# Four graph layers on one core: results of L2 and L3 used one step later, with nine and ten row buffers

## The chip, the core and the metric

The kernel runs on one core of a Trainium2 chip. A core has five engines that each work through a list of instructions in order: TensorE (PE in the profile; its weight loads are a row of their own, PEld), VectorE (DVE), ScalarE (ACT), GpSimd (POOL) and SyncE (SP). They share SBUF, on-chip memory of 128 partitions, and PSUM, into which matmuls write. They wait for each other by semaphores, which the framework places from the tiles that an instruction reads and writes. The metric is the device time of one execution, in microseconds (us).

## The reference

Node features x (6250 x 256) pass through four layers, each with its residual: h = relu(layernorm(x)), x = x + layer(h). All four share a list of 100000 edges (src, dst), sorted by dst. Only the last two layers are touched, cut here to what matters:

```
# L2: attention with one head
h   = x @ Wn.T + bn ;  e = edge_attr @ We.T + be
a   = leaky_relu(sum((h[src] + e) * attn), 0.01)          # one logit per edge
w   = exp(a - max over the edges of the same dst)
out = relu( sum over edges of w * h[src] / sum of w )      # per dst

# L3: graph convolution, with self loops
norm = deg(src)**-0.5 * deg(dst)**-0.5
out  = relu( sum over edges of (x @ W)[src] * norm + b )   # per dst
```

L0 is attention with eight heads and a feed-forward part, L1 a filtered message sum.

## The kernel before

`fast()` is the path that runs; `slow()` is the other branch of an If, for edge lists with other spacing. Nodes are padded to 49 blocks of 128. Edges are padded to 98 groups of 1024, as 8 tiles of 128 edges (J = 8). Since edges are sorted by dst, the targets of group g lie in a window of 128 nodes that begins at 64 g - 32.

Each of the stages L0 to L3 loops over the groups. For a group, POOL issues 8 indirect DMAs (`gather`, L130): each fetches, for 128 edges, the row of the source node from a table in device memory (xt2 for L2, 258 columns; xt3 for L3, 256 columns). DVE makes 8 one-hot matrices that say which target each edge has: L1095 in L2, where each row is also scaled by the edge's weight, L1150 in L3. PE multiplies one-hots with rows and adds the 8 products up in PSUM (`sum_tiles`, L681): the window sum. ACT copies it to SBUF (L691 in L2, L1175 in L3). In `sum_block` (L699) PE adds the windows that touch a block of 128 nodes, up to four, with shifted identity matrices. `blocks_done(g)` says which blocks are complete with group g: one for each even g from 2 to 96 (block 47 for 96), and block 48 for g = 97.

In L2, the weight of an edge comes from three small DVE operations, L1088 to L1090 (`al`, which read a column of the gathered rows), and an exp on ACT (L1092). A finished block goes through `out2` (L1104 to L1110): divide by the sum of weights, relu on ACT, residual, layer norm with a square root on ACT (L126), all in turns between DVE and ACT. `turned2` transposes it on PE (L1116) with a relu on ACT (L1118). `table3_row` multiplies by W on PE (L1124), scales on ACT (L1125) and writes the block's rows to xt3 with a DMA from SP (L1126). The scaled rows of all blocks also stay in SBUF, as `rows3` in the buffer `big`. exp and sqrt are in different tables of ACT; a switch is an ACT_TABLE_LOAD instruction.

In L3, `end3` (L1156 to L1159) adds the block's own row from `rows3` (the self loop), scales, adds bias and residual, and SP writes the block to the output (L1161). Every gather of L3 may read any row of xt3, so the first has to wait until L2 has written all 49 blocks.

The order of work in both loops is written out by hand under `tc.manual_schedule()`: the order in the Python code is the order of each engine's list. Step g of L2 is: gathers of group g (the first four groups are issued ahead of the loop, and ahead of an If at L1078); block sums of the blocks that were complete with g - 1; `turned2` of those complete with g - 2; weights, exp and one-hot of g; `out2` of the block summed in this same step; window sum and copy of g; `table3_row`. L3 is the same with fewer parts, and the one-hot is made a step ahead. A tile pool hands out `bufs` buffers for a tag in turn, and a new user waits until all readers of the old content are done. Row buffers: 5 groups in L2, 6 in L3. One-hots: 2. PSUM: S (window sums) 2, T (block sums) 2, B (transposes) 2, C (rows of xt3) 1. L1 gathers into twelve slices of `big` and makes the gather wait for the window sum twelve groups back (`wait_for`, L1008).

## Time and profile before

| | |
|---|---|
| median of 6 runs | 4504.04 us (4502.95 to 4508.93) |
| the profiled execution, its own time | 4501.16 us |
| its span, first to last instruction | 4499.3 us |
| busy: PE, PEld, DVE, ACT, POOL | 68%, 53%, 47%, 14%, 68% of the span |
| L2's gathers | 2497.10 to 3482.96 us |
| L3's gathers | 3501.89 to 4484.81 us |
| mean granted clock of PE | 0.826 |

A group of instructions in the profile is written as: line, engine, operation, what it writes and reads, shape, count, then busy time in us, mean ns of one, idle time of the engine just before them, and what ended most of it. "issue" means that nothing the profile shows was waited for. In a timeline, each row is the start and the length in us, and the bracket is the idle time before it with its releaser. A tile's name stands without its buffer number. Rows that were merged carry the count (x8, x16); a matrix product of 32-bit numbers shows as two passes, so that a window sum of 8 products is 16 matmuls.

### The profile page before, as it was taken

The page shows a single profiled execution, that of the slowest core. Times are in us where ns is not written, and L with a number is a line of the kernel's source. Part 1 is how long each engine was busy: PE and PEld are TensorE (multiplying, and loading weights), DVE is VectorE, ACT ScalarE, POOL GpSimd, SP SyncE. Part 2 cuts the span into 40 slices and gives each one's busy share as a digit, 9 for nine tenths or more (in the row PEclk, how much of TensorE's full clock was granted, in tenths as well). Part 3 has the DMA queues.
Part 4 walks back from the last instruction along what each step waited for, and adds up shares of the span by engine and source line. Part 5 has one row for each costly group of instructions (what it writes and reads, how often), then busy time and mean ns, then how long its engine had stood idle before and what let it go on. Part 6 is the DMA issues. An engine that isn't in the chain of part 4 may idle for free. (4 is left out here: it accounts for less than half of the span.)

```text
span 4499.3 us, 42030 instructions
## 1 busy us (share of the span) xinstructions
PE 3063.5 (68%) x12132; PEld 2375.8 (53%) x12133; DVE 2104.4 (47%) x6391; ACT 619.4 (14%) x1559; POOL 3057.5 (68%) x3215
## 2 busy tenths in 40 slices
PE   7688888888797565656566566656566555666556
PEld 4377777777645444544454345445455444444444
DVE  5476655665524566766766333333333222222222
ACT  3211010010124100000000122222222000000000
POOL 0377777777501677777777577777777677777776
PEclk9888888888898778787878688888888788788888
DMA  3365555555500344444444344444444333333333
GB/s 105 113 180 168 162 157 162 162 163 160 156 1 14 110 129 126 123 127 124 126 126 116 87 112 113 112 113 113 111 113 110 97 112 111 112 112 111 112 112 101
DMA packets 258740, 536.78 MB, mean 119 GB/s; under 512 B 65096, under 2 KB 144966, under 8 KB 258502
## 3 DMA queue, kind: packets, MB, share of 16 engines
q0 software_dynamic: 137984, 364.28, 29.8%
q1 hardware_dynamic: 107750, 156.85, 11.5%
q10 hardware_dynamic: 12768, 12.85, 0.9%
q8 instruction: 105, 1.72, 0.2%
q14 instruction: 133, 1.09, 0.1%
HBM read 504.57 MB, written 29.15 MB: 119 GB/s over the span
## 5 line engine op out<-in xcount | busy, mean ns | idle before, releaser
L130 POOL DMA_INDIRECT vg<-xt,src_i x1568 | 1489.0, 950 | 520.9 <-issue 488.3
L681 PE MATMUL ps_S<-vg,oh 128*128 128x258 f32 (+1 forms) x3136 | 988.3, 484 | 780.3 <-DMA vg<-xt,src_i 410.1
L681 PEld LDWEIGHTS ps_S<-vg,oh 128*128 128x128 f32 x3136 | 762.7, 249 | 997.8 <-issue 393.4
L130 POOL DMA_INDIRECT xbuf<-vt,src_i x784 | 782.8, 999 | 241.0 <-issue 210.4
L130 POOL DMA_INDIRECT big<-ht,src_i x784 | 742.7, 947 | 245.1 <-issue 200.0
L681 PE MATMUL ps_S<-oh,big 128*128 128x128 f32 x1568 | 308.4, 377 | 334.7 <-DVE big L1026 271.5
L1150 DVE TENSOR_SCALAR oh<-iota,rel 128x128 f32<-128x128 f32 x784 | 166.6, 301 | 740.9 <-PE ps_S L681 738.6
L681 PE MATMUL ps_S<-xbuf,oh 128*128 128x265 f32 x1568 | 486.5, 476 | 13.1 <-issue 12.1
L681 PEld LDWEIGHTS ps_S<-oh,big 128*128 128x128 f32 x1568 | 285.9, 282 | 365.3 <-DVE big L1026 236.1
L681 PEld LDWEIGHTS ps_S<-xbuf,oh 128*128 128x128 f32 x1568 | 367.6, 241 | 98.9 <-issue 16.8
L763 PE MATMUL ps_A<-scw,to 128*128 128x16 f32 x1568 | 222.5, 285 | 118.7 <-DVE to L748 118.6
L763 PEld LDWEIGHTS ps_A<-scw,to 128*128 128x128 f32 x1568 | 219.1, 222 | 137.2 <-issue 92.2
L1095 DVE TENSOR_SCALAR oh<-iota,rel,ex 128x128 f32<-128x128 f32 x784 | 215.5, 371 | 143.0 <-ACT ex L1092 143.0
L699 PE MATMUL ps_T<-ws,shifts 128*128 128x265 f32 (+2 forms) x1164 | 278.7, 382 | 0.0
L691 ACT ACTIVATE ws<-ps_S 128x265 f32<-128x265 f32 (+1 forms) x196 | 76.5, 390 | 1222.2 <-PE ps_S L681 1222.2
L699 PEld LDWEIGHTS ps_T<-ws,shifts 128*128 128x128 f32 x1164 | 220.8, 190 | 33.6
L1026 DVE TENSOR_TENSOR big<-big,ps_A 128x384 f32<-128x384 f32 (+1 forms) x294 | 132.3, 505 | 222.1 <-DMA big<-ht,src_i 220.7
L836 DVE TENSOR_TENSOR xbuf<-xbuf,ps_E 128x2048 f32<-128x2048 f32 x98 | 223.6, 2281 | 23.7 <-ACT ps_E L774 23.7
L980 PE MATMUL ps_A<-wr,rb 99*128 99x384 f32 (+1 forms) x588 | 215.3, 507 | 9.9 <-DMA rb<-in_rbf 9.9
L1088 DVE TENSOR_TENSOR al<-vg,te 128x8 f32<-128x8 f32 x98 | 16.4, 168 | 428.6 <-DMA vg<-xt,src_i 428.6
L988 DVE TENSOR_SCALAR oh<-iota,rel,cut 128x128 f32<-128x128 f32 x784 | 212.3, 362 | 0.0
L900 POOL TENSOR_TENSOR xbuf<-xbuf,bout 128x1024 f32<-128x1024 f32 (+1 forms) x13 | 29.0, 2231 | 256.1 <-ACT xn L898 249.3
(226 smaller groups left out, 3050.0 us busy)
## 6 DMA issues: line engine op xcount, KB each, us to landing
drow<-in_dst_row SPq DMA_DIRECT2D x98, 512.0 KB
ea<-in_edge_attr SPq DMA_DIRECT2D x98, 512.0 KB
vg<-xt,src_i POOLq DMA_INDIRECT x1568, 2.8
xbuf<-vt,src_i POOLq DMA_INDIRECT x784, 2.8
big<-ht,src_i POOLq DMA_INDIRECT x784, 2.6
rb<-in_rbf SPq DMA_DIRECT2D x196, 49.5 KB
vt<-row SPq DMA_DIRECT2D x49, 132.5 KB
xt<-row SPq DMA_DIRECT2D x49, 129.0 KB
```

The lines of the kernel that those rows point to most:

```text
L130: return nc.gpsimd.indirect_dma_start(out=rows, out_offset=None, in_=table, in_offset=bass.IndirectOffsetOnAxis(ap=idx[:, j:j + 1], axis=0))
L681: m = wait_for(nc.tensor.matmul(s, l, r, start=j == 0, stop=j == len(pairs) - 1), made)
L691: nc.scalar.activation(ws, s, AF.Copy)
L699: nc.tensor.matmul(t, shift_by(s), sums[g], start=i == 0, stop=i == len(parts) - 1)
L763: nc.tensor.matmul(dgs[g][:, j, :], tos[g][:, j * P:(j + 1) * P], scw[:, g // 2, g % 2, :], start=True, stop=True)
L836: made_g = nc.vector.tensor_tensor(vals, vals, ex[:, :, :, None].to_broadcast([P, J, H, HD]), OP.mult)
L900: nc.gpsimd.tensor_tensor(x[:, b0:b1, :], x[:, b0:b1, :], w1["bout"][:, None, :].to_broadcast([P, b1 - b0, D]), OP.add)
L980: filtered[g] = nc.tensor.matmul(t, rbs[g][0:33 * n, g % 2, q, :], wr3[0:33 * n, 0:n, :], start=True, stop=True)
L988: nc.vector.tensor_scalar(ohs[g][:, j, :], iota, rel[:, c], w1["cut"][:, c], OP.is_equal, OP.mult)
L1026: made_g = nc.vector.tensor_tensor(hg[:, js, :], hg[:, js, :], t, OP.mult)
L1095: made_g = nc.vector.tensor_scalar(oh[:, j, :], iota, rel[:, g * J + j:g * J + j + 1], ex[:, j:j + 1], OP.is_equal, OP.mult)
L1150: made_g = nc.vector.tensor_scalar(oh[:, j, :], iota, rel[:, g * J + j:g * J + j + 1], None, OP.is_equal)
```

## The change

In L2, a step now handles: gathers of g + 1; block sum of the blocks complete with g - 2; transposes (g - 4); product with W (g - 6); weights and one-hot of g + 1; `out2` (g - 3); window sum of g; copy of the window sum of g - 1; relu of the transposed block (g - 5); scaled row and its DMA (g - 7). In L3: gathers of g; load of the own rows of the blocks complete with g; block sum (g - 2); window sum of g; one-hot of g + 2; copy of the window sum of g - 1; `end3` (g - 3).

Rows are gathered into a list of views: three groups (L2) or four (L3) in a tile of their own, and six in `big`. A gather that reuses a view is given a wait for the last matmul of that view's window sum. `rows3` no longer exists: a block's scaled row is a tile of its own, and L3 loads the own rows back from xt3 with SP. One-hots get 4 buffers, copied window sums 8, `xn` 2. PSUM in L2: S 3, T 2, B 2, C 1, and tag A is gone, for which a branch that is not run here uses B; in L3: S 4, T 3, in a pool of its own.

The diff's core:

```diff
+        in_pool2, in_pool3, ahead = 3, 4, 4
+            room2 = ep.tile([P, in_pool2, J, TR], F32, name="vg", bufs=1)
+            views = [room2[:, i] for i in range(in_pool2)]
+            views += [big[:, i * J * TR:(i + 1) * J * TR].rearrange("p (j t) -> p j t", j=J) for i in (3, 4, 5, 0, 1, 2)]
             def rows2(g):
+                i = g % len(views)
+                vgs[g] = views[i]
+                gots[g] = [wait_for(gather(vgs[g][:, j, :], xt2, src_i[:, g * J:(g + 1) * J], j),
+                                    *([ends[g - len(views)]] if g >= len(views) else []))
+                           for j in range(J)]
...
+            def summed(g, n):
+                if g < G:
+                    wins[g] = ps("S", [P, n])
+                    oh, made_g = ohs.pop(g)
+                    ends[g] = sum_tiles(wins[g], [(oh[:, j, :], vgs[g][:, j, :]) for j in range(J)],
+                                        made_g, gots[g])
+            def taken(ep, g, n):
+                if 0 <= g < G:
+                    sums[g] = ep.tile([P, n], F32, name="ws", bufs=8)
+                    nc.scalar.activation(sums[g], wins.pop(g), AF.Copy)
...
+            def row3(b, t):
+                row = ep.tile([P, D], F32, name="row3", bufs=3)
+                nc.scalar.activation(row, t, AF.Copy, scale=dinv[:, b:b + 1])
+                nc.sync.dma_start(xt3[b * P:(b + 1) * P, :], row)
...
+                one_hot2(0)
+                for g in range(G + 7):
+                    if ahead <= g + 1 < G:
+                        rows2(g + 1)
+                    for b in blocks_done(g - 2):
+                        blocks[b] = sum_block(sums, b, TR)
+                    for b in blocks_done(g - 4):
+                        turns[b] = turned2(normed.pop(b))
+                    for b in blocks_done(g - 6):
+                        cs[b] = table3_row(b, hbs.pop(b))
+                    one_hot2(g + 1)
+                    for b in blocks_done(g - 3):
+                        normed[b] = out2(b, blocks.pop(b))
+                    summed(g, TR)
+                    taken(ep, g - 1, TR)
+                    for b in blocks_done(g - 5):
+                        hbs[b] = ep.tile([P, 2, P], F32, name="hb")
+                        nc.scalar.activation(hbs[b], turns.pop(b), AF.Relu)
+                    for b in blocks_done(g - 7):
+                        row3(b, cs.pop(b))
...
+            one_hot3(0)
+            one_hot3(1)
+            for g in range(G + 3):
+                rows3_(g)
+                for b in blocks_done(g):
+                    owns[b] = ep.tile([P, D], F32, name="own", bufs=3)
+                    nc.sync.dma_start(owns[b], xt3[b * P:(b + 1) * P, :])
+                for b in blocks_done(g - 2):
+                    blocks[b] = sum_block(sums, b, D)
+                summed(g, D)
+                one_hot3(g + 2)
+                taken(ep, g - 1, D)
+                for b in blocks_done(g - 3):
+                    end3(b, blocks.pop(b))
```

More of the change, by code (lines that the diff above doesn't have):

```diff
@@ L333, in make_windows @@
             nc.vector.tensor_reduce(lohi[:, i, :], dstf, AX.X, op)
-            t = ps("A", [P, P])
+            t = ps("B", [P, P])
             nc.tensor.transpose(t[:G, :], lohi[:, i, :], ident)
@@ L1058, in fast @@
             nc.vector.tensor_scalar(te, te, w1["ba"], None, OP.add)
-        ps = fctx.enter_context(Psum("ps2", S=2, A=1, T=2, B=2, C=1))
+        psc2 = fctx.enter_context(ExitStack())
+        ps = psc2.enter_context(Psum("ps2", S=3, T=2, B=2, C=1))
         w3 = weights(wp, "L3_gnn_W", D, D)
         brow = on_all(wp, "L3_gnn_b", D)
-        bufs2, ahead = 5, 4
+        in_pool2, in_pool3, ahead = 3, 4, 4
         with tc.tile_pool(name="e2", bufs=2) as ep:
-            vgs, gots, sums, normed = {}, {}, {}, {}
+            vgs, gots, ohs, wins, ends, sums, blocks, normed = {}, {}, {}, {}, {}, {}, {}, {}
+            room2 = ep.tile([P, in_pool2, J, TR], F32, name="vg", bufs=1)
+            views = [room2[:, i] for i in range(in_pool2)]
+            views += [big[:, i * J * TR:(i + 1) * J * TR].rearrange("p (j t) -> p j t", j=J) for i in (3, 4, 5, 0, 1, 2)]
             def rows2(g):
-                vgs[g] = ep.tile([P, J, TR], F32, name="vg", bufs=bufs2)
-                gots[g] = [gather(vgs[g][:, j, :], xt2, src_i[:, g * J:(g + 1) * J], j) for j in range(J)]
+                i = g % len(views)
[3 more added lines that the diff above has]
+                           for j in range(J)]
             with tc.manual_schedule():
@@ L1084, in one_hot2 @@
             def one_hot2(g):
+                if g >= G:
+                    return
                 gs = slice(g * J, (g + 1) * J)
@@ L1092, in one_hot2 @@
                 nc.scalar.activation(ex, al, AF.Exp)
-                oh = ep.tile([P, J, P], F32, name="oh")
+                oh = ep.tile([P, J, P], F32, name="oh", bufs=4)
                 for j in range(J):
@@ L1096, in one_hot2 @@
                                                      ex[:, j:j + 1], OP.is_equal, OP.mult)
-                return oh, made_g
+                ohs[g] = oh, made_g
+            def summed(g, n):
[8 more added lines that the diff above has]
+                    nc.scalar.activation(sums[g], wins.pop(g), AF.Copy)
             def out2(b, s):
@@ L1108, in out2 @@
                 norm_stats(b, b + 1)
-                xn = ep.tile([P, D], F32, name="xn", bufs=1)
+                xn = ep.tile([P, D], F32, name="xn", bufs=2)
                 nc.vector.tensor_scalar(xn, x[:, b, :], mv[:, b, 0:1], rstd[:, b, :], OP.subtract, OP.mult)
@@ L1116, in turned2 @@
                     nc.tensor.transpose(t[:, k, :], xn[:, k * P:(k + 1) * P], ident)
-                hb = ep.tile([P, 2, P], F32, name="hb")
-                nc.scalar.activation(hb, t, AF.Relu)
-                return hb
+                return t
             def table3_row(b, hb):
@@ L1124, in table3_row @@
                     nc.tensor.matmul(t, hb[:, k, :], w3[:, k, :], start=k == 0, stop=k == 1)
-                nc.scalar.activation(rows3[:, b, :], t, AF.Copy, scale=dinv[:, b:b + 1])
-                nc.sync.dma_start(xt3[b * P:(b + 1) * P, :], rows3[:, b, :])
-            with tc.manual_schedule():
-                for g in range(G + 2):
-                    if ahead <= g < G:
-                        rows2(g)
-                    summed = [(b, sum_block(sums, b, TR)) for b in blocks_done(g - 1)]
-                    turned = [(b, turned2(normed[b])) for b in blocks_done(g - 2)]
-                    if g < G:
-                        oh, made_g = one_hot2(g)
-                    for b, s in summed:
-                        normed[b] = out2(b, s)
-                    if g < G:
-                        sums[g], _ = sum_window(ep, oh, vgs[g], TR, made_g, gots[g])
-                    for b, hb in turned:
-                        table3_row(b, hb)
@@ L1144, in fast @@
-        with tc.tile_pool(name="e3", bufs=2) as ep, tc.manual_schedule():
-            sums = {}
+                return t
+            def row3(b, t):
+                row = ep.tile([P, D], F32, name="row3", bufs=3)
+                nc.scalar.activation(row, t, AF.Copy, scale=dinv[:, b:b + 1])
+                nc.sync.dma_start(xt3[b * P:(b + 1) * P, :], row)
+            turns, hbs, cs = {}, {}, {}
+            with tc.manual_schedule():
+                one_hot2(0)
[18 more added lines that the diff above has]
+                        row3(b, cs.pop(b))
@@ new lines, in fast @@
+        psc2.close()
+        ps = fctx.enter_context(Psum("ps3", S=4, T=3))
+        with tc.tile_pool(name="e3", bufs=2) as ep, tc.manual_schedule():
+            sums, blocks, ohs, wins, vgs, gots, ends, owns = {}, {}, {}, {}, {}, {}, {}, {}
+            room3 = ep.tile([P, in_pool3, J, D], F32, name="vg", bufs=1)
+            views = [room3[:, i] for i in range(in_pool3)]
+            views += [big[:, i * J * D:(i + 1) * J * D].rearrange("p (j t) -> p j t", j=J)
+                      for i in range(2 * NACC // (J * D))]
@@ L1147, in one_hot3 @@
             def one_hot3(g):
-                oh = ep.tile([P, J, P], F32, name="oh")
+                if g >= G:
+                    return
+                oh = ep.tile([P, J, P], F32, name="oh", bufs=4)
                 for j in range(J):
@@ L1151, in one_hot3, with rows3_ @@
                                                      OP.is_equal)
-                return oh, made_g
+                ohs[g] = oh, made_g
+            def rows3_(g):
+                if g < G:
+                    vgs[g] = views[g % len(views)]
+                    gots[g] = [wait_for(gather(vgs[g][:, j, :], xt3, src_i[:, g * J:(g + 1) * J], j),
+                                        *([ends[g - len(views)]] if g >= len(views) else []))
+                               for j in range(J)]
             def end3(b, s):
                 r0, r1 = b * P, min(N, (b + 1) * P)
-                nc.vector.tensor_tensor(s, s, rows3[:, b, :], OP.add)
+                nc.vector.tensor_tensor(s, s, owns[b], OP.add)
                 nc.vector.scalar_tensor_tensor(s, s, dinv[:, b:b + 1], brow, op0=OP.mult, op1=OP.add)
@@ L1161, in end3 @@
                     nc.sync.dma_start(out[r0:r1, :], y[0:r1 - r0, :])
-            oh, made_g = one_hot3(0)
-            for g in range(G + 1):
-                if g < G:
-                    vg = ep.tile([P, J, D], F32, name="vg", bufs=6)
-                    got = [gather(vg[:, j, :], xt3, src_i[:, g * J:(g + 1) * J], j) for j in range(J)]
-                summed = [(b, sum_block(sums, b, D)) for b in blocks_done(g - 1)]
-                if g < G:
-                    s = ps("S", [P, D])
-                    sum_tiles(s, [(oh[:, j, :], vg[:, j, :]) for j in range(J)], made_g, got)
-                    if g + 1 < G:
-                        oh, made_g = one_hot3(g + 1)
-                    sums[g] = ep.tile([P, D], F32, name="ws", bufs=6)
-                    nc.scalar.activation(sums[g], s, AF.Copy)
-                for b, s in summed:
-                    end3(b, s)
+            one_hot3(0)
[12 more added lines that the diff above has]
+                    end3(b, blocks.pop(b))
     def slow():
```

## The prediction

> **What bounds the kernel now.** I read the page's groups first, then busy time by stretch, the list of waits of POOL, and the timeline where stages meet. L2 runs from its first gather at 2497.10 to 3482.96 us, L3 from 3501.89 to the end. In the groups, POOL's row gathers are the costliest:

> ```profile
> L130 POOL DMA_INDIRECT vg<-xt,src_i x1568 | 1489.0, 950 | 520.9 <-issue 488.3
> ```

> A gather occupies POOL for 950 ns, and nearly all its idle time has "issue" as cause: no result was missing. Busy time by stretch (length, then PE, PEld, DVE, ACT, POOL with counts, clock, DMA), 300 us out of L1, L2 and L3:

> ```profile
> 1700.00:2000.00 300.00, 180.97 (x780) 141.77 (x780) 205.43 (x510) 18.77 (x75) 226.98 (x240) 0.80 0.47 126
> ...
> 2700.00:3000.00 300.00, 187.13 (x689) 149.65 (x689) 108.77 (x435) 77.03 (x150) 227.03 (x240) 0.84 0.42 113
> ...
> 3700.00:4000.00 300.00, 179.77 (x593) 141.59 (x593) 70.46 (x284) 11.17 (x30) 227.11 (x240) 0.81 0.39 111
> ```

> Each holds 240 gathers: 1.25 us apiece, 10 us a group, whatever the other engines do (PE 60 to 62% busy). POOL's list of waits has only three over 0.3 us in L2 and L3: 22.2 us ahead of L2's first gather, 18.9 ahead of L3's, and 3.1 behind the If at L1078, where POOL waits for its own 32 gathers. So inside the stages nothing is to be gained by using results later, and row buffers are not short. What can move the time is the stretch from the last landing of L2 to the first gather of L3, and that from the last landing of L3 to the end. Both are chains without a gather beside them. L2's end:

> ```profile
> 3475.31 0.17 DVE L1090 TENSOR_TENSOR al<-al,shift 128x8 f32<-128x8 f32 x1
> 3475.56 1.28 ACT L1092 ACT_TABLE_LOAD   x1 [1.41 <-DVE al L1090]
> 3476.85 0.21 ACT L1092 ACTIVATE ex<-al 128x8 f32<-128x8 f32 x1
> ...
> 3485.92 0.20 ACT L1092 ACTIVATE ex<-al 128x8 f32<-128x8 f32 x1
> ...
> 3486.15 2.14 DVE L1095 TENSOR_SCALAR oh<-iota,rel,ex 128x128 f32<-128x128 f32 x8 [0.61 <-ACT ex L1092]
> ...
> 3488.35 3.75 PE L681 MATMUL ps_S<-vg,oh 128*128 128x258 f32 x16 [1.10 <-DVE oh L1095]
> ...
> 3493.44 0.16 DVE L1104 TENSOR_SCALAR rd<-ps_T 128x1 f32<-128x1 f32 x1 [2.10 <-PE ps_T L699]
> ...
> 3498.76 0.47 ACT L1125 ACTIVATE big<-ps_C,dinv 128x256 f32<-128x256 f32 x1 [1.22 <-PE ps_C L1124]
> ...
> 3501.89 0.97 POOL L130 DMA_INDIRECT vg<-xt,src_i  x1 [18.93 <-DMA xt<-big]
> ```

> Group 96 pays 1.28 us for a table load between its logits and its exp; group 97 (from 3485.92) does not. After group 97's window sum comes block 48's chain, its row is written, and only then does POOL gather. L3's end, PE alone:

> ```profile
> 4466.67 3.69 PE L681 MATMUL ps_S<-vg,oh 128*128 128x256 f32 x16 [1.94 <-DMA vg<-xt,src_i]
> 4476.74 6.57 PE L681 MATMUL ps_S<-vg,oh 128*128 128x256 f32 x16 [6.38 <-DMA vg<-xt,src_i]
> 4483.15 1.89 PE L699 MATMUL ps_T<-ws,shifts 128*128 128x256 f32 x8
> 4486.94 3.69 PE L681 MATMUL ps_S<-vg,oh 128*128 128x256 f32 x16 [1.90 <-DMA vg<-xt,src_i]
> 4490.47 1.46 PE L699 MATMUL ps_T<-ws,shifts 128*128 128x256 f32 x6
> ```

> The same 16 matmuls take 3.69 us after 1.9 us of idle and 6.57 after 6.38. Other pairs of the stage: idle up to 2.35, 3.69; 4.55 to 4.75, 5.38 to 6.1; over 6.2, 5.2 to 6.7.

> **The change, part by part.** Sums are against the profiled execution (span 4499.3, its own time 4501.16), 2.9 us under the median of 4504.04; I add to the median.

> *Row buffers, 9 and 10, and the gather's wait for the window sum 9 or 10 groups back.* Behind a waiting gather stand all later ones on POOL's queue, and DVE's logits wait for them. But nine groups are 90 us, and a window sum is done within some 20 us of its landing: it lies some 70 us back. L1 (L1008) waits in this very form, and its 240 gathers take the same 300 us: 0.

> *Steps apart, inside a stage.* The same instructions, now a step later; POOL's 10 us a group covers them: 0. If that cover were gone, a group would cost its PE work, 187.13 / 30 = 6.2 us: still less than 10. Where a stall between PE, DVE and ACT goes, POOL is late next, as before.

> *Own rows read back in L3:* 49 more loads of 128 KB on SP, 6.3 MB beside the some 109 MB the stage moves (983 us at 111 GB/s). The last two are issued at steps 96 and 97, ahead of the last stores: 0. The row writes of L2 stay 49.

> *PSUM tags, bufs, one branch's tag in code that isn't run here:* 0, but for C, below.

> *L2's end.* Zero is the start of al(97), 3484.97. Before: one-hot made by 3.33, PE starts at 3.38, out2(48) starts at 8.47, its xn ends at 11.59, row(48) ends at 14.26, L3's gather at 16.92. After:
> 1. The out2 of a block now follows the one-hot of an even group. So the odd group's exp comes behind out2's square root and needs the table load; 97 is odd. By group 96's rows the one-hot is done 4.42 after its al, against 3.33: +1.0 at PE.
> 2. PE's queue: window sum 97 from 4.4 (16 passes at 0.216, 3.46), then block 47's sum, which used to be ahead of it (8 passes, 1.73): ready at 9.8. DVE is done with out2(46) at 7.4. out2(47) takes 3.12 (3493.44 to 3496.56 for block 48), to 12.9. Block 48's sum (behind turned2(46) and table3_row(45)) is ready at 12.4, so out2(48) starts at 12.9, not 8.47: +4.4, the 1.0 included.
> 3. C has one buffer. At step 103 table3_row(48) must wait for row3(47) of that same step. PE turns xn(48) first (done 16.5), then multiplies block 47 (1.0), ACT takes it (0.5), then block 48's product and row: done 19.6, 3.1 after the turn, against 2.2: +0.95.

> L2's end: **+5.4**. Bounds: +1.0, if only the table load is late; +6.9, if PE's window sum 97 falls into the slow clock (5.26 instead of 3.75).

> *L3's end.* Block sums move from odd steps to even ones. Window 97 thus has no block sum between it and window 96: PE idles some 6.3 us before it, and window 96 gets the warm 3.69 instead. Window 97 then takes 5.2 to 6.7, mean of such rows 5.9: +2.2 (1.5 to 3.0). Behind it PE runs block 47's sum (1.73) before block 48's, and DVE end3(47) before end3(48): block 48's y would end 1.9 later. L3's end: **+4.1**, between +1.9 (clock warm) and +4.9.

> [...]

> Sum: 5.4 + 4.1 = **+9.5, 4513.5 us** (0.21%).

> *Not shown:* gathers are 942 ns at the shortest and 950 on average; 8 x 1568 = 12.5 us is stretch, and the long ones I looked at lie beside DVE's one-hot TENSOR_SCALARs (1.02 at 4009.84 beside L1150 from 4008.96). Phases may shift it: from -12.5 to about as much more. The one-hots keep number and trigger (landing in L2, a window's end in L3), so I take 0, nearest to the row, and allow 4.

> **Rivals.**
> *Both ends mostly absorbed.* DVE and ACT catch up, the blocks' sums are ready earlier than my queue order says: 1.0 + 1.9 remain, 4507. For it: PE is idle a third of the time. Against: each engine works its list in order.
> *Not slower: the stretch goes.* Place: POOL's gathers in L2 and L3; price: all 12.5 of them; 9.5 - 12.5 = -3, 4501. It decides from 9.5 of the 12.5 on. For it: one-hots run further ahead. Against: their trigger stays tied to landings. With the lower bounds of both ends as well (2.9) it would be -9.6, 4494.
> *Gather waits aren't hidden.* A semaphore instruction on POOL's queue lasts 17 ns at the median; one for each of 1416 gathers (89 and 88 groups of 8) is +24, with the ends 4537.5. For it: each gather is handed one more wait. Against: L1's pitch of 1.25.

> **How the numbers follow.** About 0.2% (9 us) is what a measurement of this kernel can tell from no change. Forecast 0.70 (its middle lies at that bound: slower 0.41, same 0.29); absorbed 0.09 (same); stretch goes 0.08 (same 0.06, faster 0.02); waits 0.08 (slower); something not seen 0.05 (faster 0.04, slower 0.01). Faster 0.06, same 0.44, slower 0.50. Range: from absorbed less 2 of stretch, 4505, to both upper bounds (6.9 + 4.9 = 11.8) plus 4, 4520; the waits' case and most of what is unseen stay out.

> **What would show it.** Right: POOL's pitch 1.25 in both stages; a table load ahead of ex(97); idle before L3's first gather about 24.3 instead of 18.9; L3's last window over 5 us; from the last gather's start to the last y 13.6 instead of 9.5. Wrong: a pitch other than 1.25, new waits of POOL on ps_S, or ends as long as now.

## The result and the profile after

The changed kernel takes 4513.85 us (median of 18 runs, 4509.14 to 4518.51) against 4503.91 (38 runs, 4500.32 to 4509.44): +9.9 us, ratio 1.0022, 95% interval 1.0016 to 1.0028, which is +7.2 to +12.6 us. The profiled execution has a span of 4513.2 us (4499.3 before) and a mean granted clock of 0.817 (0.826 before).

First, busy time by stretch of the changed kernel, 300 us out of L2 and out of L3 (length, then PE, PEld, DVE, ACT, POOL with counts, clock, DMA):

```profile
2700.00:3000.00 300.00, 193.28 (x690) 152.36 (x690) 107.33 (x433) 72.13 (x149) 227.21 (x240) 0.82 0.42 112
3700.00:4000.00 300.00, 181.40 (x599) 143.02 (x598) 71.28 (x285) 11.49 (x30) 226.91 (x241) 0.81 0.41 118
```

The gathers come at the same pace as before, 240 and 241 in 300 us. So the stages are nearly where they were, and the two stretches without gathers must hold most of the difference. Here is L2's end in the timeline of the changed kernel, from the last rows of group 97 to L3's first gather (start and length in us, in brackets the idle time before it and its releaser):

```profile
3490.61 1.28 ACT L1103 ACT_TABLE_LOAD   x1 [4.67 <-DVE al L1101]
...
3492.15 2.14 DVE L1106 TENSOR_SCALAR oh<-iota,rel,ex 128x128 f32<-128x128 f32 x8 [1.61 <-ACT ex L1103]
...
3494.35 3.75 PE L681 MATMUL ps_S<-big,oh 128*128 128x258 f32 x16 [0.82 <-DVE oh L1106]
...
3497.94 1.90 PE L699 MATMUL ps_T<-ws,shifts 128*128 128x258 f32 x8
...
3499.88 0.16 DVE L1129 TENSOR_SCALAR rd<-ps_T 128x1 f32<-128x1 f32 x1 [2.53 <-PE ps_T L699]
...
3502.80 0.15 DVE L1129 TENSOR_SCALAR rd<-ps_T 128x1 f32<-128x1 f32 x1
...
3507.78 1.13 PE L1147 MATMUL ps_C<-l_gnn_w,hb 128*128 128x256 f32 x4 [0.56 <-ACT row L1152]
...
3509.00 0.47 ACT L1152 ACTIVATE row<-ps_C,dinv 128x256 f32<-128x256 f32 x1 [1.27 <-PE ps_C L1147]
...
3512.13 0.95 POOL L130 DMA_INDIRECT vg<-xt,src_i  x1 [24.63 <-DMA xt<-row]
```

Read it from top to bottom: a table load now stands ahead of group 97's exp; block 47's sum (3497.94) comes behind window 97, so both `out2` of blocks 47 and 48 follow one another (3499.88 and 3502.80); block 48's product waits until ACT has taken block 47's row (3507.78, "ACT row L1152"). POOL's idle time ahead of L3 is 24.63 us instead of 18.93. And L3's end, PE alone:

```profile
4487.10 5.38 PE L681 MATMUL ps_S<-big,oh 128*128 128x256 f32 x16 [2.95 <-DMA big<-xt,src_i]
4497.28 5.83 PE L681 MATMUL ps_S<-big,oh 128*128 128x256 f32 x16 [4.80 <-DMA big<-xt,src_i]
4502.95 3.19 PE L699 MATMUL ps_T<-ws,shifts 128*128 128x256 f32 x14
```

The last window takes 5.83 us instead of 3.69, and the sums of blocks 47 and 48 (8 and 6 matmuls) are one run of 14 behind it. The last gather and the last y, before:

```profile
4483.87 0.95 POOL L130 DMA_INDIRECT vg<-xt,src_i  x1 [0.30 <-issue]
...
4492.96 0.43 DVE L1159 SCALAR_TENSOR_TENSOR y<-ps_T,xbuf 128x256 f32<-128x256 f32 x1
```

and after:

```profile
4494.14 0.95 POOL L130 DMA_INDIRECT big<-xt,src_i  x1 [0.30 <-issue]
...
4507.20 0.42 DVE L1209 SCALAR_TENSOR_TENSOR y<-ps_T,xbuf 128x256 f32<-128x256 f32 x1
```

From the last gather's start to the end of the last y there are now 13.48 us, 9.52 before.

The pieces of the span, read from the traces of all the runs that follow (us; "L2" and "L3" from the first to the last gather's start, "end 2" from there to L3's first gather, "end 3" from L3's last gather's start to the end of the span, L1 for comparison, since nothing in it differs):

| kernel | L1 | L2 | end 2 | L3 | end 3 | median, ratio to before (interval) |
|---|---|---|---|---|---|---|
| before | 980.47 | 984.92 | 19.87 | 981.98 | 15.48 | 4503.91 |
| after | 981.07 | 987.16 | 25.57 | 982.01 | 19.08 | 4513.85, 1.0022 (1.0016 to 1.0028) |
| l3_only | 980.04 | 983.92 | 22.15 | 980.81 | 18.67 | 4503.25, 1.0003 (0.9994 to 1.0012) |
| few_rows | 979.48 | 985.19 | 25.69 | 981.20 | 18.51 | 4510.24, 1.0019 (1.0010 to 1.0028) |
| short_ends | 981.30 | 986.46 | 27.03 | 981.75 | 18.45 | 4508.49, 1.0017 (1.0008 to 1.0026) |
| split_before | 980.00 | 984.75 | 19.51 | 980.84 | 12.45 | 4496.18, 0.9990 (0.9981 to 0.9999) |
| l2_only | 980.82 | 985.56 | 27.06 | 983.51 | 15.55 | 4508.92, 1.0019 (1.0010 to 1.0028) |
| split_after | 982.06 | 990.09 | 25.97 | 984.64 | 13.90 | 4503.24, 1.0006 (0.9997 to 1.0016) |
| old_ends | 982.05 | 989.30 | 24.27 | 986.26 | 17.30 | 4508.53, 1.0015 (1.0006 to 1.0024) |
| split_old | 980.50 | 985.71 | 22.45 | 983.51 | 12.53 | 4503.25, 1.0007 (0.9998 to 1.0016) |

A row's pieces are of one execution, its median is of 11 or more; the profiled executions of split_after, old_ends and short_ends were the longest of their kernels (4519.11, 4519.99 and 4512.91 us), that of l3_only the shortest (4498.55). The kernel before ran beside each: 4501.74 us beside the first four experiments, 4501.25 beside the next four.

### The profile page after: what moved, and what is told of

It is laid out like the page before. It is cut to its first block, busy times and chain, and to the rows that moved or that the text cites. A ratio compares the mean times of both kernels' runs of the same rounds, so it can differ in the third digit from the quotient of the medians.

```text
span 4513.2 us, 42114 instructions
## 1 busy us (share of the span) xinstructions
PE 3091.6 (69%) x12132; PEld 2393.2 (53%) x12133; DVE 2103.1 (47%) x6391; ACT 606.1 (13%) x1557; POOL 3061.3 (68%) x3215
## 5 line engine op out<-in xcount | busy, mean ns | idle before, releaser
L130 POOL DMA_INDIRECT big<-xt,src_i x984 | 936.2, 951 | 302.5 <-issue 287.5
L130 POOL DMA_INDIRECT xbuf<-vt,src_i x784 | 783.8, 1000 | 241.1 <-issue 210.6
L130 POOL DMA_INDIRECT big<-ht,src_i x784 | 743.3, 948 | 246.3 <-issue 198.5
L681 PE MATMUL ps_S<-big,oh 128*128 128x258 f32 (+1 forms) x1968 | 579.3, 459 | 277.5 <-DMA big<-xt,src_i 226.0
L130 POOL DMA_INDIRECT vg<-xt,src_i x584 | 555.1, 950 | 222.2 <-issue 192.4
L681 PEld LDWEIGHTS ps_S<-big,oh 128*128 128x128 f32 x1968 | 458.5, 237 | 401.2 <-issue 214.4
L681 PE MATMUL ps_S<-oh,big 128*128 128x128 f32 x1568 | 309.4, 378 | 332.8 <-DVE big L1026 304.7
L699 PE MATMUL ps_T<-ws,shifts 128*128 128x265 f32 (+2 forms) x1164 | 314.8, 408 | 279.8 <-ACT ws L1122 279.8
L681 PE MATMUL ps_S<-vg,oh 128*128 128x256 f32 (+1 forms) x1168 | 354.1, 470 | 214.7 <-DMA vg<-xt,src_i 183.9
L681 PE MATMUL ps_S<-xbuf,oh 128*128 128x265 f32 x1568 | 486.6, 476 | 12.6 <-issue 12.0
L681 PEld LDWEIGHTS ps_S<-oh,big 128*128 128x128 f32 x1568 | 286.2, 282 | 363.3 <-DVE big L1026 230.2
L681 PEld LDWEIGHTS ps_S<-vg,oh 128*128 128x128 f32 x1168 | 278.9, 243 | 291.3 <-issue 177.2
L681 PEld LDWEIGHTS ps_S<-xbuf,oh 128*128 128x128 f32 x1568 | 367.9, 241 | 98.2 <-issue 15.8
L699 PEld LDWEIGHTS ps_T<-ws,shifts 128*128 128x128 f32 x1164 | 225.7, 199 | 330.3 <-ACT ws L1122 298.9
```

The lines of the kernel that those rows point to most:

```text
L130: return nc.gpsimd.indirect_dma_start(out=rows, out_offset=None, in_=table, in_offset=bass.IndirectOffsetOnAxis(ap=idx[:, j:j + 1], axis=0))
L681: m = wait_for(nc.tensor.matmul(s, l, r, start=j == 0, stop=j == len(pairs) - 1), made)
L699: nc.tensor.matmul(t, shift_by(s), sums[g], start=i == 0, stop=i == len(parts) - 1)
```

## The experiments

The theory: POOL's pace sets the stages, so the change can only move the two ends, and there it costs what each engine's list now has in another order. The rivals: the new distance or the buffers cost something inside the stages; or longer gathers (VectorE's work beside them) are the cause. "Cold" or "slow" below means that PE had half its clock for all or part of a row (granted clock 0.50 in the profile, 1.00 when warm). The diffs show an experiment's main lines against the changed kernel, that of split_before against the kernel before.

### l3_only: L2 as before, L3 as changed

```diff
+                nc.scalar.activation(rows3[:, b, :], t, AF.Copy, scale=dinv[:, b:b + 1])
...
-                one_hot2(0)
-                for g in range(G + 7):
...
+                for g in range(G + 2):
+                    if ahead <= g < G:
+                        rows2(g)
+                    summed = [(b, sum_block(sums, b, TR)) for b in blocks_done(g - 1)]
```

> L2 as before (five row tiles, PSUM as before, rows of L3's table kept in SBUF), L3 as in the changed kernel. My theory (the price lies only in the two stretches without gathers): the idle time ahead of L3's first gather goes back to about 18.9 us (24.6 in the changed kernel), the tail from L3's last gather to the last y stays near 13.5 us (9.5 before); time against the kernel before +4.0 us, ratio 1.0009 (1.0004 to 1.0014), 4508. Rival A (the step distance or the buffers cost something inside the stages): the whole +9.9 stays, or half of it by gathers and not by ends, and L3's pitch is not 1.254 us. Rival B (the stretch of L2's gathers beside VectorE's normalising made the difference): +2 or less is given back beyond the end's 5.7.

Measured: +1.5 us by the medians, ratio 1.0003 (0.9994 to 1.0012); the expected +4.0 lies in that interval, and so does nothing at all. The traces are sharper. L3's tail is 18.67, close to the changed kernel's 19.08; the idle time ahead of L3's first gather is 21.2 and not 18.9, though L2 is as before. PE's rows say why, here the last products of L2 and the last window of L3:

```profile
3491.85 2.08 PE L1126 MATMUL ps_C<-l_gnn_w,hb 128*128 128x256 f32 x4 [0.53 <-ACT hb L1120]
...
4481.21 5.38 PE L681 MATMUL ps_S<-big,oh 128*128 128x256 f32 x16 [4.88 <-DMA big<-xt,src_i]
```

The four products of block 48 took 2.08 us; in the kernel before 1.13 after the same idle time of 0.53, at a granted clock of 1.00. In the changed kernel's trace such four products, with no idle time ahead, take 1.91 us at a clock of 0.50 (2601.57) and 1.03 at 1.00 (3506.19). Window 96 in L2 took 6.44 instead of 5.26. That is 2.1 of the 2.3 us, by an estimate from these rows the clock's, in another execution of the same instructions. So an end can't be told from one execution more closely than by some 2 us. L3, the changed stage here, takes 980.81 us, so rival A is not met for L3; this run says nothing yet about L2's new form.

### few_rows: fewer row views

```diff
-            views += [big[:, i * J * TR:(i + 1) * J * TR].rearrange("p (j t) -> p j t", j=J) for i in (3, 4, 5, 0, 1, 2)]
+            views += [big[:, i * J * TR:(i + 1) * J * TR].rearrange("p (j t) -> p j t", j=J) for i in (3, 4)]
...
-                      for i in range(2 * NACC // (J * D))]
+                      for i in range(2)]
```

> The changed kernel with five row views in L2 and six in L3 instead of nine and ten, nothing else. My theory (row buffers are never waited for, POOL's pitch sets the stages): the same time as the changed kernel within 2 us, 4514, ratio to before 1.0022 (1.0015 to 1.0029), pitch 1.254 us, no wait of POOL on PE. Rival (the longer distance of the steps needs the buffers): in L2 a group's window is summed one step after its one-hot, so with five views POOL would wait on PE for up to one step of 10 us per group; already 0.1 us per group in both layers would be +20 us, 4534 or more.

Measured: 1.0019 (1.0010 to 1.0028), level with the changed kernel's 1.0022; stages 985.19 and 981.20 us, ends as in the changed kernel (25.69 and 18.51). Among POOL's waits are the one ahead of L3's first gather and those for the window sums, of which none is longer than the normal step between two gathers (in us: in total, times, longest):

```profile
POOL vg L130 <- DMA xt<-row: 24.7, 1, 24.7
...
POOL big L130 <- PE ps_S L681: 5.5, 18, 0.3
POOL vg L130 <- PE ps_S L681: 4.9, 16, 0.3
```

The nine and ten row buffers are worth nothing here, and five and six cost nothing. The rival's 0.1 us a group is excluded.

### short_ends: the last groups in another order

```diff
-                for g in range(G + 7):
+                for g in range(G - 2):
...
+                summed(G - 2, TR)
+                relu_b(h - 3)
+                row3(h - 4, cs.pop(h - 4))
...
+                one_hot2(G - 1)
+                row3(h - 2, cs.pop(h - 2))
+                normed[h - 1] = out2(h - 1, blocks.pop(h - 1))
```

(h is block 48; L3's last group is put in the order of the kernel before in the same way.)

> The changed kernel inside both layers (one step later everywhere, nine and ten views), but for the last two groups of L2 and the last group of L3 the steps are put in the order of the kernel before, with the exponential's table loaded ahead of time in L2's end. My theory: idle time ahead of L3's first gather about 18.5 us (24.6), tail after L3's last gather 9.5 to 12 us (13.5; the cold clock of the last window may stay), time 4504 to 4507, ratio to before 1.0000 to 1.0007. Rival A (the distance inside the stages costs): ratio stays above 1.0015. Rival B (gather stretch is the cause): at most +7.7 of the +9.9 goes.

Measured: 1.0017 (1.0008 to 1.0026) and an end 2 of 27.03 us. That was a miss, and my edit's fault: it put group 97's exp behind work on block 46 and on earlier blocks, on DVE's list and on ACT's. In the timeline of this kernel:

```profile
3491.10 0.41 DVE L1135 TENSOR_SCALAR xn<-xbuf,mv,rstd 128x256 f32<-128x256 f32 x1
3491.47 0.17 DVE L1099 TENSOR_TENSOR al<-big,te 128x8 f32<-128x8 f32 x1
...
3494.27 0.47 ACT L1152 ACTIVATE row<-ps_C,dinv 128x256 f32<-128x256 f32 x1 [1.00 <-ACT ws L1122]
...
3494.91 0.21 ACT L1103 ACTIVATE ex<-al 128x8 f32<-128x8 f32 x1
```

The last gather starts at 3483.91. Group 97's al starts 7.6 us after that, in the kernel before 2.95, because block 46's `out2` stands ahead of it on DVE. Its result was complete at 3492.04, and the exp starts 2.9 us later, behind a window sum's copy, two relus and two rows of the table on ACT; in the changed kernel, with its table load, it starts 1.4 later. So the larger part of the miss came from DVE's list. This run tells neither rival apart; it shows once more that the end goes by the order of one engine's list.

### split_before: the kernel before, last products freed

```diff
-                        sums[g], _ = sum_window(ep, oh, vgs[g], TR, made_g, gots[g])
+                        sums[g], _ = sum_window(ep, oh, vgs[g], TR, made_g if g < G - 1 else None, gots[g])
...
-                m = wait_for(nc.tensor.matmul(s, l, r, start=j == 0, stop=j == len(pairs) - 1), made)
-                if j == 0:
-                    wait_for(m, *got)
+                m = nc.tensor.matmul(s, l, r, start=j == 0, stop=j == len(pairs) - 1)
+                if made is not None:
+                    wait_for(m, made)
+                    if j == 0:
+                        wait_for(m, *got)
```

> The kernel before; only in the last group of L2 and of L3 the products of the window no longer wait all together for the last one-hot and the gathered rows, each waits for its own operands. My theory (the two ends are all that can be moved): the window runs beside the making of the one-hots, L2's end 1.5 to 2 us and L3's end 2 to 3 us shorter (in L3 the last window starts with its first rows), time 4499 to 4501, ratio 0.9989 to 0.9994. Rival (the ends are hidden by something else, or the products wait for the last rows anyway): no change, 4504, the idle time ahead of L3's first gather still 18.9 us.

Measured: 4496.18 us, ratio 0.9990 (0.9981 to 0.9999): inside the ratios expected, and faster than both kernels. L3's last window, PE alone:

```profile
4480.96 1.89 PE L701 MATMUL ps_T<-ws,shifts 128*128 128x256 f32 x8
4482.69 3.62 PE L681 MATMUL ps_S<-vg,oh 128*128 128x256 f32 x16
```

It follows block 47's sum without idle time and is through 3.8 us after the last gather's start, not 6.76: end 3 is 3.0 us shorter. In L2 window 97 is 1.26 us earlier, but block 48's products took 2.04 us (1.13 in the kernel before, at a clock of 1.00), so end 2 shows only 0.36 of it. This is the edit that the two ends had room for.

### l2_only: L2 as changed, L3's steps as before

```diff
-            one_hot3(1)
-            for g in range(G + 3):
+            for g in range(G + 1):
...
-                one_hot3(g + 2)
-                taken(ep, g - 1, D)
-                for b in blocks_done(g - 3):
+                one_hot3(g + 1)
+                taken(ep, g, D)
+                for b in blocks_done(g - 1):
```

> The other half: L2 as in the changed kernel, L3 with its steps in the order of the kernel before (its row views and own-row loads as in the changed kernel). My theory: L2's end as in the changed kernel, 25.6 us from L2's last gather to L3's first (19.9 before); L3's end back at 15.5 us from the last gather to the end of the span (19.1 in the changed kernel), or up to 18.5 if the last window meets a cold clock there; time +5.7 us, ratio 1.0013 (1.0005 to 1.0021). If L2's share were the rest that the run of L3 alone left by its medians, +8.4 us, ratio 1.0019. Rival (gathers inside L2 cost): a ratio over 1.002, with L2 from first to last gather more than 3 us longer than before's 984.9.

Measured: +7.7 us, 1.0019 (1.0010 to 1.0028). End 3 is back (15.55), end 2 is 27.06, because both last sets of products took longer this time:

```profile
3500.33 1.92 PE L1147 MATMUL ps_C<-l_gnn_w,hb 128*128 128x256 f32 x4
...
3502.82 2.08 PE L1147 MATMUL ps_C<-l_gnn_w,hb 128*128 128x256 f32 x4 [0.56 <-ACT row L1152]
```

The changed kernel has 1.03 and 1.13 there, at a granted clock of 1.00: +1.8, by an estimate from the rows under l3_only the clock's. The two halves, each against its own runs of the kernel before, give 7.7 + 1.5 = 9.2 us by medians, near the whole 9.9. They add up as far as intervals of 4 us to either side can show, and L2's is the larger, as predicted, by more than predicted. L2 itself, 985.56 us, is 0.6 longer than before; the rival asked for over 3. L3 is 1.5 us longer in this trace (983.51), so not all of the 7.7 need be L2's.

### split_after: the changed kernel, last products freed

The edit of split_before, at the call in `summed`.

> The changed kernel; only in the last group of L2 and of L3 the products of the window no longer wait all together for the last one-hot and the gathered rows, each waits for its own operands. My theory (the changed kernel's ends hold a last window that starts late and, in L3, at a cold clock): in L2 window 97 ends some 0.8 us after the last one-hot instead of 3.8, so the stretch to L3's first gather falls by 2 to 3 us from 25.6; in L3 the products follow the landings and the last one ends near 3.5 us after the last gather instead of 9.0, so the end falls by 5 us from 19.1; together -7 to -8, time +2 us against the kernel before, ratio 1.0004 (0.9999 to 1.0011). Rival (the ends are not what the change costs): ratio stays at 1.0022 less only L3's 2.9 us that the same edit gave in the kernel before, 1.0015 or more.

Measured: 1.0006 (0.9997 to 1.0016), some 7 us under the changed kernel: the theory's -7 to -8. But this run does not separate the theory from its rival. The rival's least, 1.0015, counted only L3's 2.9 us; the same edit gave the kernel before 0.0010 in all, so the rival would have 1.0012, which the interval holds. With the edit in both kernels the change still costs about 7.5 us (+2.0 here, -5.6 there). In L3 as expected: the window is through 3.7 us after the last gather instead of 9.0, and end 3 is 13.90 instead of 19.08. That is 5.18 us given back, 2.15 more than the 3.03 in the kernel before: the cold window's 2.14. What is left of the change's cost at the ends, 13.90 against split_before's 12.45 and 25.97 against 19.51, is 1.5 + 6.5 us, near the 7.5. In L2 the edit did less than expected: window 97 ended 1.34 us earlier (counted from its al), not 3, because it now runs straight behind window 96, which was itself late (one run of 32 matmuls on PE, 8.2 us); and none of the 1.34 is left in end 2 (25.97 against the changed kernel's 25.57). I had freed the window from its one-hots without looking at what stands ahead of it on PE.

### old_ends and split_old: a second try at the old order

```diff
-                for g in range(G + 7):
+                for g in range(G - 3):
...
+                normed[h - 2] = out2(h - 2, blocks.pop(h - 2))
+                nc.scalar.activation(ep.tile([1, 1], F32, name="early"), ident[0:1, 0:1], AF.Exp)
...
+                one_hot2(G - 2)
...
+                one_hot2(G - 1)
+                normed[h - 1] = out2(h - 1, blocks.pop(h - 1))
+                summed(G - 1, TR)
```

L3's steps are those of l2_only; split_old has the freed products besides.

> L2 one step later as in the changed kernel up to group 94, its last three groups in the order of the kernel before (window 97's exponential ahead of the work on blocks 47 and 48, the exponential's table loaded while ScalarE has nothing else), L3's steps in the order of the kernel before, nine and ten views kept. The earlier attempt at this left the last group's exponential queued behind three rows of L3's table. My theory: both ends as before (19.9 and 15.5 us; 1 to 3 us more where a window meets the cold clock), 4503 to 4506, ratio 1.0000 to 1.0006. Rival (distance and views cost something inside the stages): ratio stays over 1.0012.

> The version with old ends, and in it the last groups' products freed as in the split runs. My theory: the same gain that the split gave the kernel before, 4496 to 4499, ratio 0.9988 to 0.9995, faster than both kernels and level with the split kernel before; so the nine and ten views and the distance neither gain nor cost. Rival (the distance gains something once the ends are paid off): 4493 or less, ratio under 0.998.

Measured: 1.0015 (1.0006 to 1.0024) and 1.0007 (0.9998 to 1.0016): both missed. End 2 was 24.27 and 22.45. DVE's list shows what was late, here in old_ends:

```profile
3489.45 0.41 DVE L1135 TENSOR_SCALAR xn<-xbuf,mv,rstd 128x256 f32<-128x256 f32 x1
...
3489.82 0.17 DVE L1099 TENSOR_TENSOR al<-big,te 128x8 f32<-128x8 f32 x1
```

This is the al of group 96, not 97. It stands behind block 46's `out2`, and that was late because block 45's work, which the later order had not yet done three groups before the end, went ahead of it. In the kernel before this al comes some 6.5 us sooner, counted from the last gather. The backlog of one step that the change carries has to be worked off somewhere, and three groups are too few. So I have not shown a kernel with the changed inside and the old ends.

### caught_up, two_c, early_table, warm_l3: where POOL was held up

> L2 one step later up to group 87; at group 88 the backlog (two rows of L3's table and one block) is worked off at once, with ten groups still to gather, and the last ten groups run in the order of the kernel before; L3's steps in the order of the kernel before, nine and ten views kept. My theory: at the last gather nothing more is open than in the kernel before, so L2's end is 19.9 us again (up to 22.2, what the kernel before's own L2 gave when the clock was cold), L3's end 15.5; left over is the longer gathers beside VectorE's normalising, 1 to 2 us in L2; time +0 to +3 us, 4502 to 4505, ratio 1.0003 (0.9998 to 1.0009). Rival (the ends cannot be had back once L2 has run one step later; two attempts left ratios of 1.0015 and 1.0017): 25 us in L2's end and a ratio over 1.0012.

> The changed kernel with two PSUM buffers for L3's table rows and two for the windows of L2 (one and three before). Theory of the prediction: block 48's row no longer waits for block 47's row to leave PSUM, so its products start about 0.8 to 1.0 us earlier and the stretch from L2's last gather to L3's first falls from 25.6 to about 24.6. Rival (block 48's row waits for its own relu and products): 25.6 as before.

> The changed kernel with a one-element exponential on ScalarE straight after each block's normalising in L2, so that the exponential's table is loaded there and not ahead of the next group's own exponential. Theory of the prediction: the last group's exponential follows its input at once, not 1.3 us later, and L2's stretch from last to first gather falls by 1.0 to 1.3 us, 25.6 to 24.4; nothing changes inside L2. Rival (the load was hidden behind other work on the path): 25.6.

> The changed kernel with twelve unused passes of TensorE between L3's window 96 and its last window, so that TensorE isn't idle there; the products are used by nothing. Theory of the prediction: the last window takes 3.7 us and not 5.8, and the end of the span is 17.0 us after the last gather instead of 19.1; the rest (block 47's sum and its end ahead of block 48's) stays. Rival (the clock of that window isn't set by the idle time ahead of it): 5.4 us or more, 19 us.

caught_up works the backlog off ten groups ahead of the end:

```diff
-                for g in range(G + 7):
+                cut = G - 10
+                for g in range(cut):
...
+                for g in range(cut, G + 2):
...
+                    summed(g, TR)
+                    taken(ep, g, TR)
```

The other three are edits of the changed kernel, in the order two_c, early_table (behind every `out2`), warm_l3 (ahead of L3's last window):

```diff
-        ps = psc2.enter_context(Psum("ps2", S=3, T=2, B=2, C=1))
+        ps = psc2.enter_context(Psum("ps2", S=2, T=2, B=2, C=2))
...
+                        if g + 2 < G:
+                            nc.scalar.activation(ep.tile([1, 1], F32, name="early"), ident[0:1, 0:1], AF.Exp)
...
+                if g == G - 1:
+                    busy = ps("W", [P, D])
+                    for i in range(6):
+                        nc.tensor.matmul(busy, ident, x[:, 0, :], start=i == 0, stop=i == 5)
```

These four, the last three with one run each, ran where the kernel before itself took 5243.14 us (9 runs, 5237.64 to 5256.75). All gather stages were longer there (L1, which no edit touches, 1128 us instead of 981), POOL waited dozens of times a layer, mostly for 1 to 6 us (between its gathers in the other runs: 0.3), and at L2's last gather the windows were several groups behind. What held POOL up is not known: in L1 to L3 the profile puts most of it down to no engine of the core ("remote"). POOL's own pace did not set the stages there, so the times (5295.69, 5247.19, 5276.05 and 5269.69) don't answer what was asked. caught_up's ratio, 1.0101 (1.0088 to 1.0115), is a loss in that place only.

Two readings hold all the same, since they are within the core's own lists. In two_c, block 48's products follow block 47's at once:

```profile
4086.10 1.89 PE L1147 MATMUL ps_C<-l_gnn_w,hb 128*128 128x256 f32 x8
...
4088.08 0.47 ACT L1152 ACTIVATE row<-ps_C,dinv 128x256 f32<-128x256 f32 x1 [0.44 <-PE ps_C L1147]
```

From the end of block 48's xn to the start of its row there are 2.38 us, 3.21 in the changed kernel: 0.83 for the second PSUM buffer, as expected. The other two say nothing on their question. In early_table the table load did leave its place ahead of group 97's exp:

```profile
4082.68 0.17 DVE L1101 TENSOR_TENSOR al<-al,shift 128x8 f32<-128x8 f32 x1
4083.00 0.20 ACT L1171 ACTIVATE early<-ident 1x1 f32<-1x1 f32 x1
...
4083.99 0.19 ACT L1103 ACTIVATE ex<-al 128x8 f32<-128x8 f32 x1
```

But the exp still starts 1.14 us after its al is done, against 1.37 in the changed kernel, and not at once as expected: the early exp and three other items of ACT's list stand ahead of it. So the worth of the load in the path stays open. In warm_l3 the windows came back to back and were warm without help: 7.07 us for two, 3.62 for window 96 (in L2 of two_c 7.14 for two).

The second reading is the pace at which each order takes rows that have already landed. PE in caught_up (old order, landed rows):

```profile
4055.90 6.40 PE L681 MATMUL ps_S<-vg,oh 128*128 128x258 f32 x16 [6.94 <-DVE oh L1106]
...
4074.21 5.44 PE L681 MATMUL ps_S<-vg,oh 128*128 128x258 f32 x16 [4.22 <-DVE oh L1106]
```

and in two_c (changed order, landed rows; x32 is two windows):

```profile
4061.08 7.14 PE L681 MATMUL ps_S<-big,oh 128*128 128x258 f32 x32
...
4070.88 7.14 PE L681 MATMUL ps_S<-big,oh 128*128 128x258 f32 x32
```

Two groups take 17.3 to 18.3 us in the old order (the next pair of groups begins at 4091.54), 9.8 in the new one; 1.7 to 2.7 us of the old order's are its slow windows. That is what the change does: it nearly doubles the pace of L2's arithmetic. And it is why it gains nothing: POOL's gathers allow two groups in 20 us, and 18 was already enough.

## Why the prediction was right, and where it was not

**POOL's pace, the buffers, the steps, the own rows: 0 inside the stages.** Right for L3 (981.98 and 982.01 us) and for the buffers (few_rows). The reason given was only half of it: I set the cover at 10 us against 6.2 us of PE work a group, but the old order's own pace was 8.7 to 9.2 us a group, and the new one's 4.9. Before the change the cover was thin, about 1 us, and it held; after it, it is ample.

**The stretch of gathers: taken 0, with 4 allowed.** Mis-sized. Against L1 of the same execution, L2 is longer by 4.45, 3.88 and 4.75 us where it is as before, and by 4.74 to 8.03, mean 6.03, in the seven runs with the changed L2: +1.7 us, or +1.0 without the two longest executions (split_after and old_ends). In the changed kernel 41 of L2's gathers took 1000 ns or more, 23 of them beside DVE's xn (L1135); in the kernel before 21 and 6. In few_rows, with the same order, it was 23 and 13, so it differs between executions. The 46 gathers that overlap an xn average 1.01 us in the changed kernel, 0.98 in few_rows and 0.96 (47 gathers) in the kernel before; all others average 0.95 in each. By an estimate from these rows that is 2 us between the two kernels, about the size of the stretch. The cause, that DVE's instruction holds the gather up, is argued from their lying side by side and not tried.

**L2's end: predicted +5.4, measured +5.70**, of which 0.46 is a later landing of the last rows. Zero at the start of al(97), the steps were predicted and found at: one-hot 4.42 and 4.32; block 47's sum ready 9.8 and 9.91; `out2(48)` 12.9 and 12.83; row(48) ended 19.6 and 19.50; L3's gather 22.3 and 22.16. Of its parts, the wait for C was 0.95 and measured 0.83 by taking it away; the table load is in the trace, and its effect on the path by itself was not settled. By medians L2's half is +7.7 (4.5 to 12.6): end, stretch, and the clock's share, which differs from execution to execution.

**L3's end: predicted +4.1, measured +3.96** to the last y: 2.14 for the cold window (predicted 2.2) and 1.75 for block 47's sum and end (predicted 1.9). One detail failed: "window 96 gets the warm 3.69 instead". It took 5.38 after 2.95 us of idle, and the idle time ahead of window 97 was 4.80, not 6.3. The step assumed that a short idle time makes a warm window, and the phase decides that too (below). The kernel before had the rows against it, left out of the prediction's list of pairs: 12 of its last 24 odd windows took 5.2 to 5.4 us after 2.4 to 3.3 us of idle. And the size of the clock's part was that of one execution. Over the last 48 groups of L3, odd windows average 4.52 us before and 5.92 after: the cold window costs 1.4 us on average, not 2.1.

**The sum.** The two profiled spans differ by 13.9 us: 5.70 and 3.60 at the ends, 2.24 in L2's stage, 0.03 in L3's, and 2.3 ahead of L2, where nothing that runs differs. So the change's part of this pair is some 11.6 us, or 11.0 with the mean 1.7 for the stretch, against +9.9 by medians, within the interval's 2.7 us. That 9.5 came so near to 9.9 is in part luck: the stretch's 1.7 was left out, and the clock's part was 0.8 larger than its average. Of the rivals, the waits of the gathers are excluded: L3 takes as long as before, and the trace has no more semaphore instructions on POOL at the gathers' line (645, before 652), so the rival's one for each gather was not there to pay. The stretch went the other way. And the ends were not absorbed: they grew by 5.70 and 3.96 us, step by step as written down.

What stays open: what the table load alone is worth in L2's end, and whether the changed L2 with really old ends runs level with the kernel before. Two orders missed it, and the third ran where POOL did not set the pace.

## What to carry to other kernels

Before giving every result one more step of distance, find which list sets the pace of the stage. If an engine with no waits does (here POOL, 10 us a group), the distance buys nothing inside and is paid at the stage's last group, where the backlog is worked off with nothing beside it. The same place is where gains are: freeing the last group's products from the wait for its last one-hot and all its rows took 0.1% off the kernel before, with no other change.

## What the runs showed of the hardware

*The clock beats with the groups.* In L3's PE rows the same 16 matmuls take 3.69 us for some groups and 5.1 to 6.7 for others. From the changed kernel, even and odd windows in turn:

```profile
4386.93 3.69 PE L681 MATMUL ps_S<-big,oh 128*128 128x256 f32 x16 [2.07 <-DMA big<-xt,src_i]
4396.93 6.50 PE L681 MATMUL ps_S<-big,oh 128*128 128x256 f32 x16 [6.30 <-DMA big<-xt,src_i]
...
4416.97 6.72 PE L681 MATMUL ps_S<-big,oh 128*128 128x256 f32 x16 [6.37 <-DMA big<-xt,src_i]
```

The granted clock over the first two is 1.00 and 0.56. From 4446.98 on (group 92), even windows took 5.4 instead, after some 3 us of idle, much as from groups 58 and 76 on: the pattern comes back after 18 and 16 groups. The kernel before shows the same beat with odd and even exchanged; in the changed kernel no odd window from group 3 on was under 5.07. By these rows the last window of L3 has the clock that its phase gives it. The runs have several: old_ends had 5.38 after 2.43 us of idle, short_ends 6.39 after 5.18, l2_only 3.69 after 1.99.

*A table load lets the next activation start at once.* In the changed kernel each of 99 loads took 1.28 us (1283 ns). In L2's end one starts at 3490.61, and the exp started at 3491.91, 11 ns behind it; all loads but the first have 11 or 12 ns there. Nor was there a pause ahead of the load where ACT came straight from other work: one load starts at 3483.44, 18 ns after an activation that ran from 3482.97 for 0.45 us.
